# Queries loaded two chunks ahead and a group's first keys used last: an attention and expert kernel on one Trainium2 core

## The chip, the cores and the metric

The kernel runs on one core of one Trainium2 chip. The metric is device time in microseconds (us) of one launch. A core has a matrix engine (PE, with its weight loads shown apart as PEld), a vector engine (DVE), a scalar engine (ACT), a general engine (POOL) and SyncE (SP), which here issues nearly all DMA transfers. Each engine works through its own instructions in order.

## The reference, cut to what matters

The input `x` has 2048 tokens of 512 features. It is normalised (`xn`), and the output is `x + attention(xn) + experts(xn)`. Attention is the part that the change touches: 16 heads, each with two sets of queries and keys of depth 16 and one set of values of depth 32, a causal mask, two softmaxes.

```python
q = (query @ Wq).reshape(bsz, tgt_len, 2 * H, D)      # k likewise, then rotary on both
v = (query @ Wv).reshape(bsz, tgt_len, H, 2, D)
...
def causal_attn_pair(q, k, v1, v2, mask, scale):
    s = jnp.einsum('bthd,bshd->bhts', q, k) * scale
    s = jnp.where(mask, s, NEG)
    a = jax.nn.softmax(s, axis=-1)
    o1 = jnp.einsum('bhts,bshd->bthd', a, v1)
    o2 = jnp.einsum('bhts,bshd->bthd', a, v2)
    return jnp.concatenate([o1, o2], axis=-1)
...
attn = irfft((rfft(attn1) - lambda_full * rfft(attn2)) * filt)   # along the tokens
attn = attn * rsqrt(mean(attn * attn) + EPS) * rms_weight * (1.0 - LAMBDA_INIT)
return attn @ Wout
```

The expert part is a gated two-layer network: every token goes through a shared expert and through the two of eight routed experts that its gate chooses.

## The kernel before

Three stages follow each other. The opening normalises, projects to queries, keys and values, turns queries and keys by the rotary angles, routes the tokens, and writes queries and keys to two arrays in device memory, `parts[0]` and `parts[1]`. `middle` computes all of attention and nearly all of the expert work. `ending` does the filter along the tokens, the normalisation, the last projection and the sum.

**Groups, chunks, units.** `middle` works on two heads at a time, a group `g`, of which there are 8. A group has four chunks of 512 queries, taken from the last to the first: `qc` = 3, 2, 1, 0 (list `turns`, line 989). Because of the mask, chunk `qc` needs only the keys 0 to 512(qc + 1). Keys are kept in four column blocks `c` of 512 keys, each with a tile per head. A block holds four key tiles of 128, numbered `kb`, so `kb // 4` is the block. A unit is one head against one `kb`: two matmuls (line 831) into PSUM, then an exponential on ACT (line 844). `units` (lines 805 to 818) gives the order inside a chunk: first `LEAD[qc]` whole key tiles (0, 0, 2, 6 for the four chunks) and the first tile of the diagonal, then the rest of the diagonal, whose masking POOL does (line 853), then the whole tiles that are left. A chunk `qc` = 3 has 29 units, the others 21, 13 and 5, and 68 make a group.

**The order of the work.** All engines run in the order in which the program is written (`manual_schedule`). The loop at line 1038 takes four units at a time. `burst` issues the score matmuls of two of them; the product with the values (line 875), the sums of the last chunk (line 901), and one or more steps of expert work (`work`, line 1026, from the generator `experts`, line 626) follow, in the same instruction stream of PE. Expert weights are fetched by SP (line 151) as soon as the matmuls that used a buffer are issued.

**Loads of queries and keys.** `load_queries` (line 739) issues 8 transfers of 64 KB into two tiles, one per head; a tag has two buffers. `load_keys` (line 728) issues 4 transfers of 128 KB, two per head; each writes the same 32 source rows twice, through a source with a leading dimension of 2. Block 0 has four buffers, two groups' worth; blocks 1, 2 and 3 have two. Before the loop (lines 997 to 1000) SP gets all four blocks of group 0 and the queries of its first chunk. After that, at the start of every chunk, `burst` (lines 1008 to 1014) has SP load the next chunk's queries, and then one block of the next group's keys, `(qc + 1) % 4`: block 0 in chunk 3, block 3 in chunk 2, block 2 in chunk 1 and block 1 in chunk 0. SP takes these in turn with everything else in its stream, and it waits where a buffer is still being read. Eight completion semaphores serve SP's transfers in rotation, so that a transfer also waits for the one issued eight before it.

Of the kernel before, what the change touches and what calls it, by code (L numbers as in the profile page):

```python
# [9 lines left out]
F32R = mybir.dt.float32r  # L10
# [9 lines left out]
P = 128  # L20
# [5 lines left out]
QC = 512  # L26
NQC = T // QC
TQ = QC // P
NH = 16
NG = NH // 2  # L30
# [4 lines left out]
LEAD = (0, 0, 2, 6)  # L35
# [35 lines left out]
def block_kernel(  # L71
# [220 lines left out]
    with ExitStack() as pools:  # L292
        def pool(name, bufs, **kw):
            return pools.enter_context(tc.tile_pool(name=name, bufs=bufs, **kw))
# [219 lines left out]
        qp, ep = pool("qk", 2), pool("early", 2)  # L514
# [78 lines left out]
    def middle(general):  # L593


        with ExitStack() as pools:
# [8 lines left out]
            def pool(name, bufs, **kw):  # L605
                return pools.enter_context(tc.tile_pool(name=name, bufs=bufs, **kw))

            kp, qp, pp = pool("k", 2), pool("q", 2), pool("prob", 6 if general else 8)
# [118 lines left out]

            def load_keys(g, c):
                for h in (2 * g, 2 * g + 1):
                    k = kp.tile([P, QC], F32R, tag=f"k{c}", name="kS", bufs=4 if c == 0 else 2)  # L730
                    for s in range(2):
                        src = parts[1][2 * h + s, :, :, c * QC : (c + 1) * QC].rearrange("a d t -> (a d) t")
                        nc.sync.dma_start(
                            k[64 * s : 64 * s + 64, :].bitcast(F32),
                            src.unsqueeze(0).to_broadcast([2, 2 * D, QC]),
                        )
                    keys[h, c] = k

            def load_queries(g, qc):
                for h in (2 * g, 2 * g + 1):  # L740
                    q = qp.tile([P, QC], F32R, tag=f"q{h % 2}", name="qS")
                    for s in range(2):
                        for rep in range(2):
                            r = 64 * s + 32 * rep
                            nc.sync.dma_start(
                                q[r : r + 32, :].bitcast(F32),
                                parts[0][2 * h + s, rep : rep + 2, :, qc * QC : (qc + 1) * QC].rearrange("a d t -> (a d) t"),
                            )
                    queries[h, qc] = q
# [48 lines left out]
            class Chunk:  # L798
# [6 lines left out]
                def units(self):  # L805


                    d = self.qc * TQ
                    for kb in [*range(LEAD[self.qc]), d]:
                        for h in range(2):  # L810
                            yield [(h, kb, 0, 0, QC)]
                    for h in range(2):
                        yield [(h, d + 1, P, 0, 3 * P), (h, d + 3, 3 * P, 3 * P, P)]
                    last = [(h, d + 2, 2 * P, 2 * P * h, 2 * P) for h in range(2)]
                    yield from ([part] for part in last) if general else [last]
                    for kb in range(LEAD[self.qc], d):
                        for h in range(2):
                            yield [(h, kb, 0, 0, QC)]

# [44 lines left out]
                def values(self, kb):  # L864

                    if self.done == 0:
                        self.o = vps.tile([P, QC], F32, tag="o", name="ps_o")
                    self.done += 1
                    first, self.ended = self.done == 1, self.done == (self.qc + 1) * TQ
                    for h in range(2):  # L870
                        v0 = 64 * self.g + 32 * h
                        pt, off = self.probs[h, kb]
                        for s in range(2):
                            r = 64 * h + 32 * s
                            nc.tensor.matmul(  # L875
                                self.o[r : r + 32, off:], vd[:, kb, v0 : v0 + 32], pt[:, s, :],
                                start=first, stop=self.ended, skip_group_check=True,
                            )
                    if self.ended:
                        self.o_sb = ap.tile([P, QC], F32, tag="o_sb", name="o_sb")  # L880
                        nc.scalar.copy(self.o_sb, self.o)
# [107 lines left out]
            turns = [(g, qc) for g in range(NG) for qc in reversed(range(NQC))]  # L989
            stream = []  # L990
            for n, turn in enumerate(turns):
                chunk = Chunk(*turn)
# [3 lines left out]
            ex = experts()  # L996
            for c in range(NQC):
                load_keys(0, c)
                if c == 0:
                    load_queries(0, NQC - 1)  # L1000
            worked, begun, summed, held = 0.0, -1, 0, []
            todo, closing, closed, shared, ready, folding = [], [], [], [], [], None

            def burst(units):
                nonlocal begun
                found = []
                for n, chunk, unit in units:
                    if n > begun:
                        begun = n
                        if n + 1 < len(turns):  # L1010
                            load_queries(*turns[n + 1])

                        if chunk.g + 1 < NG:
                            load_keys(chunk.g + 1, (chunk.qc + 1) % NQC)
                    found += chunk.scores(unit)
                return found

# [20 lines left out]
            for i in range(0, len(stream), 4):  # L1038
                units = stream[i : i + 4]
                found = burst(units[:2])  # L1040
                n, ended = values()
                for c in closing:
                    c.sums()
                    summed += 1
                if n < 2 and not closing:

                    work()
                found += burst(units[2:])
                while todo:
                    ended += values()[1]  # L1050
# [20 lines left out]
                if any(masked(*u[1:]) for u in units) or not shared:  # L1071
                    steps = 0
                elif any(masked(*u[1:]) for u in stream[i + 4 : i + 8]):
                    steps = 1 if ready or units[0][1].g == NG - 1 else 0
                else:
                    steps = 2
# [269 lines left out]
    with tc.If(nc.values_load(more[0:1, 0:1], min_val=0, max_val=1) > 0):  # L1346

        with tc.tile_pool(name="before_more", bufs=1) as gap, tc.tile_pool(name="more", bufs=2) as mp, tc.tile_pool(
            name="more_ps", bufs=3, space=PSUM
# [24 lines left out]
    with tc.If(flag > 0) as cmp:  # L1374
        middle(False)
        ending()
    with cmp.Else():
        middle(True)
        ending()
# [103 lines left out]
```

## Time and profile before

| What | Value |
|---|---|
| median of 3 runs | 1334.18 us (1333.29 to 1334.27) |
| the profiled execution's own time | 1336.14 us |
| its span | 1334.3 us |
| PE busy | 1305.5 us, 98% of the span |
| DVE busy | 1007.7 us, 76% |
| ACT busy | 690.5 us, 52% |
| POOL busy | 620.3 us, 46% |
| key loads `kS<-parts_k` | 128 transfers of 128 KB |
| query loads `qS<-parts_q` | 256 transfers of 64 KB |
| expert weights `w<-in_wex_dram` | 132 transfers of 704 or 768 KB |

Times in the profile are counted from the start of the span. `middle`'s first score matmul stands at 254.0 us and its last at 1199.7 us. A busy PE in this profile means that an instruction is in it; a wait of PE for a semaphore is idle time, and the profile says which engine or transfer ended it. The trace also holds, for each transfer, when SP issued it and when its last part landed. "PEclk" is the clock that PE was granted, as a share of full speed.

### The profile page before, as it was taken

Reading aid. Unit: us, or ns where it says so; the run is one execution under the profiler, and the core shown is the slowest. Engines: PE = TensorE matmul, PEld = TensorE weight load, DVE = VectorE, ACT = ScalarE, POOL = GpSimd, SP = SyncE. Lnnn points to the kernel's source line nnn. Section 1 sums busy time; section 2 is a strip of 40 time slices with the busy share of each in tenths; the row PEclk is TensorE's granted clock in tenths of the full one; section 3 lists DMA queues with packets and bytes.
Section 4 is the critical chain, followed back from the end, with each engine's and each line's share of the span. In section 5 each row is a group of like instructions: output and inputs, shape, how many; then the busy total and the mean of one; then the engine's idle time right before and its main releaser. Section 6 shows DMA issues by size and latency. Waiting matters only on the chain.

```text
span 1334.3 us, 20914 instructions
## 1 busy us (share of the span) xinstructions
PE 1305.5 (98%) x7554; PEld 598.5 (45%) x7554; DVE 1007.7 (76%) x1316; ACT 690.5 (52%) x848; POOL 620.3 (46%) x639
## 2 busy tenths in 40 slices
PE   7999999999999999999999999999999999999998
PEld 3444444434343444444445444444544443445544
DVE  7049883277777868778987988888798869876784
ACT  2311110265666566666666666666666657662231
POOL 0002331012131233215985976894598666741774
PEclk9999999999999999999999999999999999999999
DMA  9405773201210023235566666566666667878998
GB/s 371 184 16 163 201 205 102 89 16 32 66 63 22 29 78 93 77 111 160 169 186 202 183 196 188 149 215 191 170 199 189 191 186 271 314 266 304 190 222 188
DMA packets 82058, 215.07 MB, mean 161 GB/s; under 512 B 12964, under 2 KB 13416, under 8 KB 81688
## 3 DMA queue, kind: packets, MB, share of 16 engines
q1 hardware_dynamic: 69224, 186.47, 43.9%
q0 software_dynamic: 11056, 22.78, 8.7%
q10 hardware_dynamic: 1664, 4.38, 1.0%
q8 instruction: 63, 1.03, 0.4%
q14 instruction: 51, 0.42, 0.1%
HBM read 170.48 MB, written 43.10 MB: 160 GB/s over the span
## 4 chain that ended last, share of the span: by engine, by line
PE 64%; POOL 8%; DMA 5%; issue 2%; DVE 2%; ACT 0%; SPq 0%; POOLq 0%; DVEq 0%; ACTq 0%
PE ps_o L875 17%; PE ps_s L831 12%; PE wh L244 8%; PE xy L214 6%; PE xh L181 5%; PE xg L181 5%; PE wy L283 4%; POOL res L1138 3%; DMA res<-ysh 2%; PE ps_sum L901 2%; DMA w<-in_wex_dram 1%; PE ps_x L167 1%; POOL pt L853 1%; DVE sum L892 1%; PE ps_ot L913 1%
## 5 line engine op out<-in xcount | busy, mean ns | idle before, releaser
L892 DVE TENSOR_TENSOR sum<-sum,pt 128x1024 f32<-128x1024 f32 (+2 forms) x576 | 628.7, 1140 | 30.4 <-POOL pt L853 13.6
L844 ACT ACTIVATE pt<-ps_s 128x1024 f32<-128x1024 f32 x544 | 527.3, 1022 | 182.5 <-PE ps_s L831 127.3
L853 POOL TENSOR_SCALAR_AFFINE_SELECT pt<-pt 128x256 f32<-128x256 f32 (+1 forms) x224 | 164.4, 756 | 368.4 <-ACT pt L844 342.9
L875 PE MATMUL ps_o<-pt,vd 128*32 128x512 f32 (+3 forms) x2560 | 267.7, 534 | 1.9 <-POOL pt L853 1.9
L831 PE MATMUL ps_s<-qS,kS 64*128 64x512 f32 (+3 forms) x1280 | 204.5, 407 | 1.6 <-DVEq L1346 1.2
L831 PEld LDWEIGHTS ps_s<-qS,kS 64*128 64x128 f32 x1280 | 97.5, 185 | 177.3 <-issue 96.7
L244 PE MATMUL wh<-xnT,w 128*128 128x512 f32 (+1 forms) x352 | 150.4, 574 | 0.0
L875 PEld LDWEIGHTS ps_o<-pt,vd 128*32 128x32 f32 x2560 | 67.2, 109 | 123.3 <-issue 105.9
L495 POOL DMA_INDIRECT who<-pairs,slot x32 | 33.8, 1055 | 171.3 <-DVE pairs L492 104.3
L542 PE MATMUL ps_x<-xnT,wqk_sb 128*128 128x512 f32 x256 | 110.5, 593 | 0.0
L244 PEld LDWEIGHTS wh<-xnT,w 128*128 128x128 f32 x352 | 64.1, 190 | 72.6 <-issue 56.5
L214 PE MATMUL xy<-w,uT 128*128 128x512 f32 (+3 forms) x240 | 94.6, 599 | 1.2 <-DVE rcp L916 1.2
L181 PE MATMUL xh<-w,xT 128*128 128x352 f32 (+1 forms) x320 | 90.4, 477 | 4.0 <-DMA w<-in_wex_dram 3.2
L181 PE MATMUL xg<-w,xT 128*128 128x352 f32 (+1 forms) x320 | 88.6, 468 | 0.0
L930 POOL TENSOR_TENSOR vd<-o_n 128x128 f32<-128x128 f32 x60 | 58.1, 986 | 53.8 <-DVE o_n L921 53.7
L542 PEld LDWEIGHTS ps_x<-xnT,wqk_sb 128*128 128x128 f32 x256 | 48.4, 190 | 60.6 <-issue 60.6
L283 PE MATMUL wy<-w,ws 128*128 128x512 f32 x160 | 74.8, 603 | 0.0
L559 ACT CAST hi<-turned 128x1024 fp32r<-128x1024 f32 x16 | 16.7, 1045 | 93.9 <-DVE turned L557 59.3
L1138 POOL DMA_INDIRECT res<-ys,slot x32 | 53.3, 1667 | 23.7 <-DMA res<-ysh 11.7
L181 PEld LDWEIGHTS xh<-w,xT 128*128 128x128 f32 (+1 forms) x320 | 48.3, 178 | 31.0 <-issue 9.3
L181 PEld LDWEIGHTS xg<-w,xT 128*128 128x128 f32 (+1 forms) x320 | 46.6, 174 | 34.4 <-issue 14.8
L377 PE MATMUL ps_tv<-wv_sb,xnT 128*128 128x512 f32 x128 | 59.8, 620 | 0.7 <-ACT xnT L374 0.7
(252 smaller groups left out, 1368.4 us busy)
## 6 DMA issues: line engine op xcount, KB each, us to landing
w<-in_wex_dram SPq DMA_DIRECT2D x88, 704.0 KB
w<-in_wex_dram SPq DMA_DIRECT2D x44, 768.0 KB
kS<-parts_k SPq DMA_DIRECT2D x128, 128.0 KB
qS<-parts_q SPq DMA_DIRECT2D x256, 64.0 KB
ys<-y_sb SPq DMA_DIRECT2D x34, 256.0 KB
parts_q<-hi SPq DMA_DIRECT2D x32, 256.0 KB
parts_k<-hi SPq DMA_DIRECT2D x16, 256.0 KB
parts_k<-turned SPq DMA_DIRECT2D x16, 256.0 KB
```

The costliest lines, as they stand in the source:

```text
L181: nc.tensor.matmul(dst[r, :], xT[:, c, r], w[:, c * FI : (c + 1) * FI], start=(c == 0), stop=(c == NE - 1), skip_group_check=True,)
L214: nc.tensor.matmul(y[r, :], uT[:m, ic, r], w[:m, ic * E : (ic + 1) * E], start=(ic == 0), stop=(ic == NF - 1), skip_group_check=True,)
L244: nc.tensor.matmul(dst, w_sb[o // WUP][o % WUP // WONE][:, o % WONE : o % WONE + P], x[:, c, :], start=(c == 0), stop=(c == NE - 1),)
L283: nc.tensor.matmul(y, us[i][:, t * P : (t + 1) * P], w_sb[i // NF][2][:, i % NF * E : (i % NF + 1) * E], start=(i == 0), stop=(i == SCH - 1),)
L377: nc.tensor.matmul(pv, xnT[:, c, t * P : (t + 1) * P], wv_sb[:, c, :], start=(c == 0), stop=(c == NE - 1))
L542: nc.tensor.matmul(ps[:, i, :], wqk_sb[st, qk][:, i, c, :], xnT[:, c, cols], start=(c == 0), stop=(c == NE - 1),)
L831: nc.tensor.matmul(to, k, queries[2 * g + h, qc][r, off : off + w], start=True, stop=not general)
L844: nc.scalar.activation(pt[:, :, used], ps[:, :, used], AF.Exp, scale=SCALE)
L853: nc.gpsimd.affine_select(out=part, in_=part, pattern=[[0, part.shape[1]], [1, P]], compare_op=ALU.is_ge, fill=0.0, base=0, channel_multip ...
L875: nc.tensor.matmul(self.o[r : r + 32, off:], vd[:, kb, v0 : v0 + 32], pt[:, s, :], start=first, stop=self.ended, skip_group_check=True,)
L892: nc.vector.tensor_add(to, to, pt)
L1138: nc.gpsimd.indirect_dma_start(out=came[k], out_offset=None, in_=ys, in_offset=bass.IndirectOffsetOnAxis(ap=slot[:, step - 2, order[k] : o ...
```

## The change

Queries: three buffers per tag instead of two, and at the start of chunk `n` SP loads the queries of chunk `n + 2` instead of `n + 1`. The queries of the second chunk are loaded ahead of the loop, after key block 1.

Keys: block 0 has two buffers like the others. In a chunk `qc` = 3 the whole key tiles are taken in the order 4 to 11, then 0 to 3, so that block 0 is the last that the chunk uses, from its 22nd unit on. Block 0 of a group is loaded at the start of that group's own chunk 3 (for group 0 ahead of the loop, as before) and no longer at the start of chunk 3 of the group before. The other blocks are loaded where they were. The number of buffers for keys and queries together stays at 14.

```diff
             def load_keys(g, c):
                 for h in (2 * g, 2 * g + 1):
-                    k = kp.tile([P, QC], F32R, tag=f"k{c}", name="kS", bufs=4 if c == 0 else 2)
+                    k = kp.tile([P, QC], F32R, tag=f"k{c}", name="kS")
...
             def load_queries(g, qc):
                 for h in (2 * g, 2 * g + 1):
-                    q = qp.tile([P, QC], F32R, tag=f"q{h % 2}", name="qS")
+                    q = qp.tile([P, QC], F32R, tag=f"q{h % 2}", name="qS", bufs=3)
...
                     d = self.qc * TQ
-                    for kb in [*range(LEAD[self.qc]), d]:
+
+                    kbs = [*range(TQ, d), *range(TQ)] if self.qc == NQC - 1 else [*range(d)]
+                    for kb in [*kbs[: LEAD[self.qc]], d]:
                         for h in range(2):
                             yield [(h, kb, 0, 0, QC)]
...
-                    for kb in range(LEAD[self.qc], d):
+                    for kb in kbs[LEAD[self.qc] :]:
                         for h in range(2):
                             yield [(h, kb, 0, 0, QC)]
...
             for c in range(NQC):
                 load_keys(0, c)
-                if c == 0:
-                    load_queries(0, NQC - 1)
+                if c < 2:
+                    load_queries(0, NQC - 1 - c)
...
                         begun = n
-                        if n + 1 < len(turns):
-                            load_queries(*turns[n + 1])
-
-                        if chunk.g + 1 < NG:
-                            load_keys(chunk.g + 1, (chunk.qc + 1) % NQC)
+                        if n + 2 < len(turns):
+                            load_queries(*turns[n + 2])
+
+                        c = (chunk.qc + 1) % NQC
+                        g = chunk.g + (c > 0)
+                        if 0 < g < NG:
+                            load_keys(g, c)
                     found += chunk.scores(unit)
```

## The prediction

> **What bounds the kernel now.** I read the page's busy times first, then the stage between 254 and 1205 us, then PE's waits in it.
>
> ```profile
> PE 1305.5 (98%) x7554; PEld 598.5 (45%) x7554; DVE 1007.7 (76%) x1316; ACT 690.5 (52%) x848; POOL 620.3 (46%) x639
> ```
>
> ```profile
> 254.00:1205.00 951.00, 943.57 (x6428) 425.50 (x6432) 771.95 (x898) 614.91 (x733) 513.66 (x543) 1.00 0.48 150
> ```
>
> In the second fence the first number after the window is its length, the next PE's busy time: 7.4 us of 951 idle. PE sets the time of this stage, and each us that it comes to wait is a us of the kernel. The waits of PE in that window are few:
>
> ```profile
> PE xh L181 <- DMA w<-in_wex_dram: 3.2, 2, 2.1
> PE ps_o L875 <- POOL pt L853: 1.9, 3, 1.4
> PE ps_s L831 <- DVEq L1346: 1.2, 1, 1.2
> PE xy L214 <- DVE rcp L916: 1.2, 1, 1.2
> ```
>
> No row says that PE waited for queries (qS) or keys (kS). So the change has no wait to remove there; the question is whether it makes one. For this I read SP's order of transfers around a group's end, here group 3's chunk 0 and group 4's chunk 3, and where PE starts on the latter:
>
> ```profile
> 713.25 8.74 SPq L745 DMA_DIRECT2D qS<-parts_q  x8
> 722.04 2.20 SPq L733 DMA_DIRECT2D kS<-parts_k  x4
> ```
>
> ```profile
> 724.91 0.73 PE L831 MATMUL ps_s<-qS,kS 64*128 64x512 f32 x4
> ```
>
> The columns are start, length, engine and line. The four kS transfers of 722 us are block 1 of group 4, issued at the start of the short chunk 0 (5 units), because chunk 1 was the last to read the old block 1. Group 4's first scores come 2.9 us later. Today they read block 0, loaded a hundred us before.
>
> **What the Trainium skill says.** "DMA: Bandwidth & Descriptors", section "Why a DMA increments its semaphore by 16 and not by 1": a transfer uses as many of the 16 DMA engines as divide its slowest dimension on both sides, up to 16. A key load's source has a leading dimension of 2, hence two engines. The trace agrees. While SP's queue held keys alone, from about 228 us, the rate stayed near 50 GB/s, in slices of 0.65 us (the peaks are stores that POOL issued):
>
> ```profile
> GB/s 44 47 22 91 32 50 50 47 47 50 50 50 50 50 54 50 41 28 25 47 54 340 114 50 50 54 47 50 173 284 50 76 57 44 50 50 211 246 50 50
> ```
>
> 128 KB at 50 GB/s is 2.6 us, and the landing records of that load stand 2.6 us apart (232.2, 234.8, 237.4 us). Four take some 10.5 us, however free the other engines are. The same page, "Queues, rings and completion order", has each DMA engine take its queue's work in order, so a block of keys also holds up the first two engines for every transfer behind it. "TensorE: Matmul & The Clock Gate", "Part 1: The HAM clock gate", says that an idle window of about 3.4 us halves PE's clock and a busy one restores it. The trace has one case, at the only wait of PE for weights:
>
> ```profile
> 1092.50:1096.50 4.00, 1.03 (x5) 0.19 (x3) 3.86 (x6) 1.05 (x2) 2.57 (x2) 0.92 0.50 129
> 1096.50:1102.50 6.00, 5.81 (x18) 2.20 (x18) 0.67 (x3) 0.53 (x2) 3.65 (x4) 0.50 0.52 154
> ```
>
> The third number from the right is the granted clock: after 3.15 us of idleness, 6 us at 0.50, that is 3 us lost on top.
>
> **The change part by part, against the profiled 1336.14 us (span 1334.3; 0.15% above the median of 1334.18).**
>
> *Queries two chunks ahead.* From the trace's landing records the tightest queries before are those of each group's chunk 3, ready for the first head 2.1 to 8.7 us ahead of use. They were never late, so nothing is gained: 0. SP's stream keeps 8 query transfers at each chunk start, with other contents, waiting for the same matmuls: the buffer they take was that of the chunk just finished, as now. Only the last load (8 transfers at 1170.6 us) moves away and 8 come in ahead of the loop. There block 1 keeps its place (landed 240.7, used from 254.0); blocks 2 and 3 slip by about 1.5 us of query data (8 x 0.19 us, the spacing of query landings), from 252.4 and 264.5 us, against a use at 269.6 and 276.4. Hidden by 10 us or more; without that cover, at most the 1.5 us.
>
> *Block 0 in two buffers, loaded in its own chunk 3.* This adds a wait of SP on the matmuls of the chunk 0 just ended, but the queries in front of it wait for the same ones. Behind it stand a result store and the down weights (w2), as before: every chunk 3 but the last had four kS there already. Its use comes at the 22nd unit. Laid over the trace, block 0 would land 2.9 us (group 4) to 19.6 us (group 1) before that, more after any delay of PE: 0. In group 7 the load is new in its place. Behind it a w2 transfer, which landed at 1106.2 us for a use at 1111.6, comes some 10.5 us later, at about 1117. By itself that would cost 5 us. The delay below moves the use to about 1121, so I put 0.
>
> *Block 1 first.* This is the step that counts. With order 4 to 11, then 0 to 3, the first two units of chunk 3 read block 1, one head each. Block 1 is still loaded at the start of chunk 0, behind 8 query transfers. It used to be needed from the 9th unit on (key tile 4), with 2.8 to 11.6 us to spare for the second head. Now it is needed by the 1st and 2nd. PE executes in order, so the values product, the sums and the expert work behind those two units wait as well. The stall is the landing of the second head's keys less the start of the second unit, both from the trace:
>
> group 1: 381.0 - 375.8 = 5.2; group 2: 503.6 - 497.3 = 6.3; group 3: 616.3 - 608.6 = 7.7; group 4: 738.0 - 725.2 = 12.8; group 5: 854.4 - 841.3 = 13.1; group 6: 975.7 - 963.0 = 12.7; group 7: 1092.3 - 1079.6 = 12.7. Sum 70.5 us. With 0.1 us each from landing to matmul (1094.71 to 1094.84 at the weights' wait), 71 us. Group 0 has its block early. The later groups stall longer because expert weights are on the queue.
>
> *The clock.* Seven stalls of over 5 us. The one case cost 3 us; by the page a release takes one to two windows of 3.4 us at half clock, so 1.7 to 3.4 us each. I take 2.6: 18 us.
>
> *What comes back.* The weights' wait at 1092.8 to 1096.7 falls into group 7's stall: 3.15 + 3 = 6 us. The short waits inside chunks 3 (ACT xT 0.7 at 614, DVE rcp 1.2 at 847, POOL pt 1.9) go, as those engines catch up: 3.5 us. Late next is PE itself again.
>
> *Sum.* 71 + 18 - 6 - 3.5 = 79.5, on the profiled time 1416, on the median 1334.2 + 79.5 = 1414 us. Instruction counts on all engines are unchanged.
>
> **Rivals.**
> (a) *Shorter stalls.* In the later groups the second head's keys needed 8 us for two transfers (729.9 to 738.0), not 5.2, as weights that SP issued behind them were moving too. Where PE's stall holds those weights back, about 3 us less in each of four groups, and the clock at its low end (-6): 1414 - 12 - 6 = 1396. For it: weights are issued when PE has read the old ones. Against: most were issued before the stall begins (726.3 us for 724.9, freed by matmuls at 722.5).
> (b) *Longer ones.* Clock at its high end (+6), no recovery of short waits (+4), w2 late in group 7 (+5): 1429.
> (c) *Faster.* If block 1 landed before the chunk, only the relief would be left: block 0 no longer queued ahead of other groups' needs, and the wait of 6 us for weights at 1094 gone. 1334.2 - 6 = 1328. It decides if the four kS of block 1 take less than the 2.7 to 8 us between their issue and the first scores; 128 KB would have to land in under 0.7 us in the later groups, where the trace shows 2.6. Or the compiled program would have to move the load; its SP order in the changed program still has it behind the queries at the start of chunk 0, and its first score matmuls of a group still wait for it.
> (d) *No difference.* Slower and faster parts would have to cancel, or the order in the chunk would have to be other than the diff says. Nothing in the instruction order supports it.
>
> **How the numbers follow.** Main case with (a) and (b) as its ends: 0.94. (c) 0.03, (d) 0.03. A measurement of this kernel tells about 0.2% (2.7 us) from no change. Faster 0.03, same 0.03, slower 0.94. The range, 1395 to 1431, is (a) to (b) and a little beyond; what it leaves out is (c), (d) and a misjudged stall.
>
> **What would show it.** In the profile after: PE ps_s waiting for kS, seven times, some 70 us in sum, 5 to 13 us each, right at the start of chunks 3 of groups 1 to 7 and none in group 0; a granted clock of 0.5 for some us after each; no wait of xh for weights near group 7; PE's busy time up by the clock's share, other engines' busy times unchanged. I am wrong if PE doesn't wait there, if the keys are issued earlier than the queries of chunk 0, or if kS transfers take far less than 2.6 us.

## The result and the profile after

| | before | changed |
|---|---|---|
| median | 1333.74 us (4 runs) | 1416.89 us (1415.65 to 1420.32, 4 runs) |
| ratio to before | | 1.0628, 95% interval 1.0608 to 1.0647 |
| span of the profiled execution | 1334.3 us | 1418.6 us |

The change makes the kernel 83 us slower. One run of the kernel before (1866.59 us, granted clock 0.66) and one of the kernel with the keys ahead of the queries (1650.37 us, 0.75) were in a slower state and are left out below. First the busy times of the changed kernel's page, and the row of the granted clock in 40 equal slices of the span:

```profile
PE 1330.0 (94%) x7554; PEld 606.0 (43%) x7554; DVE 1008.5 (71%) x1316; ACT 690.9 (49%) x848; POOL 630.8 (44%) x639
...
PEclk9999999999999999989997999799989989999999
```

The instruction counts are those of before. PE's busy time grew by 24.5 us though it does the same work, and the clock row has dips at near regular distances. DVE and ACT are unchanged. The stage that held 7.4 us of idle PE time now has 66. In this row the window is followed by its length, the busy times of PE, PEld, DVE, ACT and POOL, the granted clock, the DMA engines' busy share and GB/s, and the idle time is the length less PE's busy time:

```profile
254.00:1288.00 1034.00, 968.22 (x6425) 432.79 (x6428) 773.04 (x898) 615.28 (x733) 520.25 (x542) 0.96 0.45 137
```

The waits of PE between 370 and 1170 us (columns: total us, times, longest) say for what:

```profile
PE ps_s L833 <- DMA kS<-parts_k: 52.9, 21, 5.0
PE ps_s L833 <- issue: 9.0, 3, 4.1
PE ps_o L877 <- POOL pt L855: 1.8, 2, 1.6
PE xh L181 <- ACT xT L169: 0.7, 1, 0.7
```

Line 833 is the score matmul (831 before). It waits for keys, which it did nowhere before, for 61.9 us: the three waits of the second row stand between waits of the first at the same places. The wait of xh for weights is gone (xh and xg are an expert's two input products, xy its output product). One group's start, on PE, shows how a wait goes. This is group 4, whose block 1 SP issued at 747.2 us, behind the queries:

```profile
738.70 8.42 SPq L745 DMA_DIRECT2D qS<-parts_q  x8
747.16 2.38 SPq L733 DMA_DIRECT2D kS<-parts_k  x4
```

```profile
751.99 0.47 PE L833 MATMUL ps_s<-qS,kS 64*128 64x512 f32 x1 [1.56 <-DMA kS<-parts_k]
754.52 0.79 PE L833 MATMUL ps_s<-qS,kS 64*128 64x512 f32 x1 [2.06 <-DMA kS<-parts_k]
758.94 0.76 PE L833 MATMUL ps_s<-qS,kS 64*128 64x512 f32 x1 [3.63 <-DMA kS<-parts_k]
763.66 0.76 PE L833 MATMUL ps_s<-qS,kS 64*128 64x512 f32 x1 [3.96 <-DMA kS<-parts_k]
764.35 4.49 PE L877 MATMUL ps_o<-pt,vd 128*32 128x512 f32 x32
```

The first two units of the chunk are four matmuls, and each waits for the next of the four key transfers. PE gets on at 764.35 us. The 32 instructions of the values product behind took 2.36 us at this place before (from 725.58 us) and take 4.49 here. The reason is the clock, the third number from the right in these windows of the same execution:

```profile
757.00:764.40 7.40, 1.50 (x6) 0.62 (x10) 0.00 (x0) 0.00 (x0) 0.00 (x0) 0.50 0.71 176
764.40:770.00 5.60, 5.60 (x61) 2.81 (x64) 0.00 (x0) 1.61 (x2) 0.00 (x0) 0.50 0.27 79
770.00:776.00 6.00, 6.00 (x49) 3.04 (x45) 4.21 (x7) 3.68 (x5) 2.95 (x4) 1.00 0.34 63
```

For 5.6 us after the stall PE works all the time at half clock, then at full.

### The profile page after: what moved, and what is told of

It reads as the page before. It is cut to its first block, busy times and chain, and to the rows that moved or that the text cites. A ratio compares the mean times of both kernels' runs of the same rounds, so it can differ in the third digit from the quotient of the medians.

```text
span 1418.6 us, 20879 instructions
## 1 busy us (share of the span) xinstructions
PE 1330.0 (94%) x7554; PEld 606.0 (43%) x7554; DVE 1008.5 (71%) x1316; ACT 690.9 (49%) x848; POOL 630.8 (44%) x639
## 4 chain that ended last, share of the span: by engine, by line
PE 57%; DMA 13%; POOL 9%; issue 2%; SPq 1%; DVE 0%; ACT 0%; POOLq 0%; ACTq 0%; DVEq 0%
PE ps_o L877 16%; PE ps_s L833 11%; PE wh L244 7%; DMA kS<-parts_k 7%; PE xy L214 5%; PE xg L181 4%; PE xh L181 4%; PE wy L283 4%; DMA w<-in_wex_dram 3%; POOL res L1142 3%; PE ps_sum L903 2%; DMA res<-ysh 1%; POOL pt L855 1%; PE ps_ot L915 1%; PE ps_x L167 1%
## 5 line engine op out<-in xcount | busy, mean ns | idle before, releaser
L877 PE MATMUL ps_o<-pt,vd 128*32 128x512 f32 (+3 forms) x2560 | 281.4, 558 | 2.7 <-POOL pt L855 2.6
L833 PE MATMUL ps_s<-qS,kS 64*128 64x512 f32 (+3 forms) x1280 | 217.5, 411 | 63.5 <-DMA kS<-parts_k 52.9
L833 PEld LDWEIGHTS ps_s<-qS,kS 64*128 64x128 f32 x1280 | 101.9, 186 | 247.2 <-issue 142.0
L877 PEld LDWEIGHTS ps_o<-pt,vd 128*32 128x32 f32 x2560 | 70.1, 113 | 133.5 <-issue 115.7
L542 PE MATMUL ps_x<-xnT,wqk_sb 128*128 128x512 f32 x256 | 110.5, 593 | 0.0
L918 DVE RECIPROCAL rcp<-ps_st 128x16 f32<-128x16 f32 x32 | 8.3, 260 | 137.4 <-PE ps_st L916 137.4
L181 PE MATMUL xh<-w,xT 128*128 128x352 f32 (+1 forms) x320 | 86.8, 462 | 0.8 <-ACT xT L169 0.7
```

The lines of the kernel that those rows point to most:

```text
L181: nc.tensor.matmul(dst[r, :], xT[:, c, r], w[:, c * FI : (c + 1) * FI], start=(c == 0), stop=(c == NE - 1), skip_group_check=True,)
L542: nc.tensor.matmul(ps[:, i, :], wqk_sb[st, qk][:, i, c, :], xnT[:, c, cols], start=(c == 0), stop=(c == NE - 1),)
L833: nc.tensor.matmul(to, k, queries[2 * g + h, qc][r, off : off + w], start=True, stop=not general)
L877: nc.tensor.matmul(self.o[r : r + 32, off:], vd[:, kb, v0 : v0 + 32], pt[:, s, :], start=first, stop=self.ended, skip_group_check=True,)
```

## The experiments

The theory: block 1 became the first block that chunk 3 reads and lands too late, because it is issued late and moves on two DMA engines; each stall also costs some slow clock. The rivals: the query loads do it; the two-buffer block 0 does it; the growth of PE's busy time is something other than the clock. Ratios are to the kernel before as it ran beside each experiment (medians of 1334.4 to 1335.4 us).

**The keys' part alone.**

```diff
-                    q = qp.tile([P, QC], F32R, tag=f"q{h % 2}", name="qS", bufs=3)
+                    q = qp.tile([P, QC], F32R, tag=f"q{h % 2}", name="qS")
...
-                        if n + 2 < len(turns):
-                            load_queries(*turns[n + 2])
+                        if n + 1 < len(turns):
+                            load_queries(*turns[n + 1])
```

> The changed kernel with the queries put back (two buffers, loaded one chunk ahead); the keys' part of the change stays. Theory (block 1 is now the first block that a group's chunk 3 reads and lands 5 to 13 us too late): the stalls stay, 1417 us, within 4. Rival (the third query buffers and the longer reach of the query loads crowd SP's queue, so that keys and weights come late): the time falls back towards 1334, at least half of the 83 us goes.

Measured: 1417.08 us, ratio 1.0617 (1.0598 to 1.0636), PE busy 1329.5 us. That is the changed kernel's time within the noise: beside the keys' part, the queries' part costs nothing and brings nothing, and all of the loss comes from the keys' part.

**Block 2 first.**

```diff
-                    kbs = [*range(TQ, d), *range(TQ)] if self.qc == NQC - 1 else [*range(d)]
+                    kbs = [*range(2 * TQ, d), *range(TQ, 2 * TQ), *range(TQ)] if self.qc == NQC - 1 else [*range(d)]
```

> The changed kernel with one list reordered: chunk 3 takes key tiles 8 to 11, then 4 to 7, then 0 to 3, so that block 2 (loaded two chunks earlier) is read first and block 1 from the 9th unit on, as before the change. Loads, buffers and SP's order are those of the changed kernel. Theory: no wait of PE for keys is left, the clock stays at full, 1334 us (1328 to 1340). Rival (the two-buffer block 0 or the query loads cost the time): stays above 1375.

Measured: 1346.49 us, ratio 1.0093 (1.0075 to 1.0111). The reordered list takes away 70 of the 83 us, so the order in the chunk is the cause of these, and neither block 0's buffers nor the queries are. The expectation missed by 6 us at its upper end. PE's waits in this kernel, in the middle stage:

```profile
PE xy L214 <- DMA w<-in_wex_dram: 7.5, 1, 7.5
PE xh L181 <- DMA w<-in_wex_dram: 3.5, 2, 2.9
PE ps_o L877 <- POOL pt L855: 1.9, 3, 1.4
```

No keys, but a new wait of xy for down weights, 7.5 us long. It stands in group 7's chunk 3, where SP has this order (same kernel):

```profile
1082.53 17.81 SPq L745 DMA_DIRECT2D qS<-parts_q  x8
1100.38 2.19 SPq L733 DMA_DIRECT2D kS<-parts_k  x4
1102.68 1.98 SPq L226 DMA_DIRECT2D ys<-y_sb  x1
1104.91 4.54 SPq L151 DMA_DIRECT2D w<-in_wex_dram  x5
```

The kS there are block 0 of group 7, new in this place. By the landing records the last of them came at 1117.3 us and the first of the weights behind at 1119.4, 14.5 us after its issue; before, the weights at this place needed 4.8 us. PE started on them at 1119.48, and its clock stayed at half until 1125.4, 6 us in which it did what full clock does in 3:

```profile
1119.50:1125.40 5.90, 5.90 (x16) 1.80 (x16) 0.00 (x0) 0.51 (x1) 0.00 (x0) 0.50 0.14 55
```

So the wait cost some 7.5 + 3 us of the 12; the rest isn't traced.

**Only that block cut up.** In the kernel with block 2 first, block 0 of group 7 is loaded in transfers of 32 rows, two for each of before.

```diff
+                        if (g, c) == (NG - 1, 0):
+                            for r in (64 * s, 64 * s + 32):
+                                nc.sync.dma_start(k[r : r + 32, :].bitcast(F32), src)
+                        else:
...
```

> The kernel with block 2 read first, with one block of keys alone, block 0 of group 7, cut into transfers of 32 rows. Theory (its four transfers hold two DMA engines in front of group 7's down weights, which cost that kernel 7.5 us of waiting and 5 us of slow clock): the wait of xy for weights goes, the wait of xh for weights at 1094 us stays; 1334 us (1331 to 1338). Rival (the down weights are late from the queries in front of them): 1344 or more.

Measured: 1338.02 us, ratio 1.0020 (1.0011 to 1.0028), just at the upper end of what was expected. The wait of xy is gone, and that of xh stays:

```profile
PE xh L181 <- DMA w<-in_wex_dram: 4.0, 2, 2.9
PE ps_o L881 <- POOL pt L859: 1.9, 3, 1.4
```

Eight of the 12 us went with four transfers' shape; the queries in front of the weights are as before, so the rival falls. It lies 3 us above the kernel before (1335.37 us beside it). The wait of xh is 0.8 us longer than there, and its trace has a period of 3.4 us at half clock at 255 us that the others lack; the rest stays open.

**Keys ahead of the queries.**

```diff
-                        if n + 2 < len(turns):
-                            load_queries(*turns[n + 2])
-
                         c = (chunk.qc + 1) % NQC
                         g = chunk.g + (c > 0)
                         if 0 < g < NG:
                             load_keys(g, c)
+                        if n + 2 < len(turns):
+                            load_queries(*turns[n + 2])
```

> The changed kernel with the two loads at a chunk's start exchanged: the keys are issued ahead of the 8 query transfers, so some 4 us earlier in groups 1 to 3 and some 8 us earlier in groups 4 to 7. Theory: the stalls fall from 63 us to about 23 (0, 1, 4, 5, 4, 4, 6 us), with perhaps half of the slow-clock time; 1364 us (1350 to 1380). Rival (the keys' own transfer time alone sets the landing, the queries ahead of them are cheap): 1405 or more.

Measured: 1362.92 us (median of three runs), ratio 1.0223 (1.0201 to 1.0245). The wait for keys, 61.9 us in the changed kernel, is

```profile
PE ps_s L833 <- DMA kS<-parts_k: 16.9, 9, 2.7
```

The place in SP's queue was worth 54 us. That the rest is the transfers' own time isn't shown by this run; the kernels with cut transfers below bear it out.

**Useless matmuls in the stall.**

```diff
+FILL = (0, 23, 29, 37, 54, 46, 51, 55)
...
+                    if qc == NQC - 1 and g > 0 and unit[0][:2] == (0, TQ):
+                        for i in range(FILL[g]):
+                            nc.tensor.matmul(ps[:, i % 2, :C_TRI], ident, cst, start=True, stop=True)
```

> The changed kernel with useless matmuls (identity by 224 constant columns, into PSUM that the scores then overwrite) ahead of the first unit of chunk 3 in groups 1 to 7: 23, 29, 37, 54, 46, 51 and 55 of them, some 0.19 us each, a little less than each stall. They add work to the outputs' computation that changes nothing in it. Theory (some 27 us of the loss is PE's halved clock after each stall): the stalls stay as filled time, the clock stays at full, 1390 us (1385 to 1400). Rival (the growth of PE's busy time has another cause, such as contention): 1417 or above.

Measured: 1440.13 us, ratio 1.0792 (1.0773 to 1.0811). By the time alone this is the rival's range, but the edit was mis-sized, so the time can't decide. In the groups of this kernel, with shapes kept apart,

```profile
L831 PE MATMUL ps_s<-cst 128*128 128x224 f32 x590 | 112.9, 353 | 0.0
```

295 calls became 590 instructions, so that a filling took 0.38 us and not 0.19, and the filling outlasted every stall. Even so its busy time answers the rival. No wait for keys was left, and the clock stayed at full through the middle stage:

```profile
254.00:1310.00 1056.00, 1052.10 (x7042) 535.48 (x7046) 774.02 (x899) 614.96 (x734) 520.28 (x542) 1.00 0.43 135
```

PE's busy time, 1413.1 us, is that of the kernel with cut transfers below (1302.6) plus 110.5. The filling accounts for that (112.9, in part at the same time as the matmuls beside it), so with the clock at full the growth is gone.

**Half the filling.** `FILL = (0, 11, 14, 18, 26, 23, 25, 27)`.

> As the run with useless matmuls, with 11, 14, 18, 26, 23, 25 and 27 of them: there each took 0.38 us and not 0.19 (two PE instructions each), so the filling was longer than the stalls and set the time itself. Theory (slow clock): the filling now fits in the stalls, the clock stays at full, and what is left of the loss is the stalls alone: 1334.7 + 62.7 (stalls of the changed kernel) - 6 (the weights' wait and its slow clock) = 1391 us (1386 to 1398). Rival (PE's busy time grows for another cause): 1415 or more.

Measured: 1409.06 us (1405.16 to 1410.05), ratio 1.0560 (1.0539 to 1.0581). Adding work made the kernel 8 us faster, as the clock theory has it, but by less than expected: it lies between the theory's range and the rival's. In the middle stage the time at half clock fell from 89 us to 14 us in the traces. The expectation had taken all of PE's growth in busy time as lost time. Part of it lies inside the stalls, where matmuls run slow between two waits and cost nothing. Take the stretch from the start of the last matmul ahead of a group's first scores (the filling not counted) to the start of the first behind its first two units. Summed over groups 1 to 7, the trace has 83.1 us for the changed kernel, 78.9 here and 8.6 with cut transfers. So the stalls are 70 us at nearly full clock and 75 with the slow clock in them.

**Block 1 a group early.** The queries go back to two buffers; block 1 gets four.

```diff
-                    k = kp.tile([P, QC], F32R, tag=f"k{c}", name="kS")
+                    k = kp.tile([P, QC], F32R, tag=f"k{c}", name="kS", bufs=4 if c == 1 else 2)
...
-                        if 0 < g < NG:
+                        if 0 < g < NG and c != 1:
                             load_keys(g, c)
+                        if chunk.qc == 2 and chunk.g + 1 < NG:
+                            load_keys(chunk.g + 1, 1)
```

> The changed kernel with the queries put back (two buffers, one chunk ahead) and the four key tiles that this frees given to block 1, which is then loaded at the start of the chunk 2 of the group before. 14 tiles in all, as in both kernels; no keys are loaded in the short chunk 0. Theory: no wait for keys, the weights' wait of the last groups goes with the keys that stood in front of them in chunk 0 of group 6; 1328 us (1325 to 1333). Rival (block 0 of group 7 in front of the weights costs its 12 us here too): 1338 to 1346.

Measured: 1354.39 us, ratio 1.0142 (1.0120 to 1.0164). Both expectations missed. No wait for keys is left, but these came:

```profile
PE ps_s L833 <- DMA qS<-parts_q: 8.2, 6, 3.0
...
PE xh L181 <- DMA w<-in_wex_dram: 4.4, 1, 4.4
PE xy L214 <- DMA w<-in_wex_dram: 3.0, 1, 3.0
```

Eight key transfers in a row at the start of chunk 2 made all that followed late. In group 3, SP finished issuing the queries of chunk 0 at 702.3 us and block 2 began then:

```profile
691.76 10.54 SPq L745 DMA_DIRECT2D qS<-parts_q  x8
702.35 2.36 SPq L733 DMA_DIRECT2D kS<-parts_k  x4
```

In the kernel before, the same kS began at 696.3 us. The 6 us went on to the next queries, those of group 4's chunk 3, which landed at 729.7 us and not 723.6, and had only 1 to 2 us to spare there. Two chunks of lead, which this kernel doesn't have, might have covered that; no run tried it.

**Cut transfers in the changed kernel.**

```diff
-                        nc.sync.dma_start(
-                            k[64 * s : 64 * s + 64, :].bitcast(F32),
-                            src.unsqueeze(0).to_broadcast([2, 2 * D, QC]),
-                        )
+                        for r in (64 * s, 64 * s + 32):
+                            nc.sync.dma_start(k[r : r + 32, :].bitcast(F32), src)
```

> The changed kernel with each key transfer of 128 KB cut into two of 64 KB whose source has 32 rows (no leading dimension of 2), so that by the Trainium skill each uses 16 DMA engines; order and buffers unchanged. Theory (two engines make the keys late): a block lands some 6 us after its first issue and not 13 to 14, the stalls fall to 0 in groups 1 to 3 and to 2 or 3 us in groups 4 to 7; 1336 us (1328 to 1346). Rival (the place in SP's queue is the cause, and more transfers make it worse): 1390 or more.

Measured: 1329.99 us (1329.27 to 1331.52, 8 runs), ratio 0.9965 (0.9953 to 0.9977). All 87 us go with the shape of the key transfers, and the kernel is a little faster than before as well. The completion records show the difference in engines: of the changed kernel's 128 key transfers 122 have three increments of their semaphore, one 0.4 us after the issue and two as the data lands; of the 256 cut ones 254 have sixteen. The same place as above, group 4's block 1:

```profile
712.98 4.77 SPq L743 DMA_DIRECT2D qS<-parts_q  x8
717.80 3.68 SPq L734 DMA_DIRECT2D kS<-parts_k  x8
```

The eight land between 719.8 and 722.9 us, some 0.45 us apart, 1.9 us after the last issue; PE wants them at 724.65. The queries ahead of them are also through sooner (4.8 us against 8.4), as nothing in front of them stands on two engines. In the changed kernel it was 16 us from the first key issue to the last landing. PE's waits in the middle stage are back to small ones:

```profile
PE ps_o L875 <- POOL pt L853: 2.6, 4, 1.4
PE ps_s L831 <- DVEq L1348: 1.3, 1, 1.3
PE xy L214 <- DVE rcp L916: 0.9, 1, 0.9
PE xh L181 <- ACT xT L169: 0.7, 1, 0.7
PE ps_s L831 <- DMA kS<-parts_k: 0.3, 1, 0.3
```

**Cut transfers in the kernel before.** The same edit.

> The kernel before with the same cut of the key transfers, nothing else. Theory: its one wait of PE for weights (3 us and 3 us of slow clock) goes, as keys no longer hold up two of the engines: 1328 us (1326 to 1331). Rival (that wait comes from the volume of the weights): no change, 1334.

Measured: 1330.10 us, ratio 0.9964 (0.9951 to 0.9977). The wait for weights is gone here too, so it was the keys in front of them and not the weights' volume. The longest entry of PE's waits in the middle stage is now

```profile
PE ps_o L873 <- POOL pt L851: 2.7, 4, 1.4
```

With the cut, the order of before and the order of the change give the same time, with PE busy for 98% of either span.

**Cut transfers for block 1 alone,** in the changed kernel (`if c == 1` in the edit above).

> The changed kernel with block 1's loads alone cut into transfers of 32 rows. Theory: the 62 us of waits at the starts of chunk 3 go but for about 3 us in each of groups 4 to 7, where the queries in front are still held up by block 2's two-engine transfers; with the slow clock of those, and up to 12 us for group 7's weights behind block 0, 1350 us (1338 to 1362). Rival (all key transfers share in the loss, not block 1's landing): above 1375.

Measured: 1348.96 us, ratio 1.0087 (1.0064 to 1.0111). PE waits 5.4 us for keys in all, and 3.7 us for down weights:

```profile
PE ps_s L837 <- DMA kS<-parts_k: 5.4, 9, 1.4
PE xy L214 <- DMA w<-in_wex_dram: 3.7, 1, 3.7
```

68 us go with the shape of block 1's transfers alone. The other 19 of the 87 go with the other blocks' shape, as the kernel with all of them cut shows; the wait for down weights is one place where they cost, and the rest isn't split up.

**Block 1 a group early, with cut transfers.** Both edits together.

> The kernel that loads block 1 a group early, which waited for queries and weights instead, with all key transfers cut into 32 rows. Theory (8 key transfers at the start of a chunk 2 hold two DMA engines for 21 us and pass their delay down the queue to the queries of the next chunks, which had only 2 us to spare): no wait for queries or weights, 1330 us (1327 to 1334), the same as the other kernels with cut transfers. Rival (the place of the loads in SP's stream is the cause): 1345 or more.

Measured: 1330.48 us, ratio 0.9956 (0.9943 to 0.9970), no wait for queries or weights in the middle stage. The 24 us that the early loads cost go with the shape of the key transfers as well.

## Why the prediction was right

The mechanism came as predicted: the waits, their places, the half clock behind them, and none in group 0. The sum was 79.5 us; the medians differ by 83 and the spans of the profiled executions by 84.3. In the prediction's own terms the 84.3 are 74.5 for stalls, plus 15.4 for the clock, less 5.6 for what comes back. The stalls were put too low by 3.5, the clock too high by 2.6, and the relief too high by 3.9. That the total is off by 4.8 and not by 7.4 is luck.

*The stalls.* Predicted 71 us. Measured as the stretches above, changed kernel less cut transfers: 5.6, 6.6, 8.4, 13.3, 14.1, 13.3, 13.2, together 74.5 us, of which 61.9 are idle and the rest matmuls between the waits. Each is 0.3 to 1.0 us longer than predicted. The lateness of a moved use could be read off a trace in which nothing waited. Rival (a), shorter stalls because weights are held back, didn't come.

*The clock.* Predicted 18 us for seven stalls. Between the spans of the changed kernel and of that with cut transfers (1418.6 and 1328.7) lie 89.9 us, 15.4 more than the stretches. The trace says the same another way. Behind the ends of the seven stalls the clock stayed at half for 3.4, 3.2, 4.9, 5.6, 5.6, 5.4 and 2.8 us, together 30.9, and half of that is lost: 15.5 us, or 2.2 per stall and not 2.6. The filling gained 8 us in the median and 15 between the two profiled executions; the one is the fastest of its four runs and the other the slowest.

The Trainium skill, "TensorE: Matmul & The Clock Gate", section "Part 1: The HAM clock gate", has windows of about 3.4 us by which the clock is set, and the trace's periods of half clock agree (6.8, 6.8, 10.2, 17.1, 17.1, 17.1 and 13.7 us). The prediction's "one to two windows" is an estimate from that page. On one point the measurement goes further than the page's "idle window": in the 3.4 us ahead of the seven drops of the clock PE was busy for 1.2, 0.7, 0.7, 1.4, 0.0, 1.3 and 0.5 us. So a stall that is broken up by single matmuls halved the clock too, and in group 1 no gap was longer than 2.2 us. The clock came back only after 3.4 us in which PE never idled.

*What comes back.* Predicted 6 + 3.5 us (its three short waits add up to 3.8). The weights' wait and its slow clock went. The short waits mostly didn't: in the middle stage POOL's rose from 1.9 to 2.6 and xT's stayed at 0.7; only rcp's 1.2 is gone. The step that failed is that other engines' catching up would clear them. The kernel with cut transfers, which has no stalls, is 5.6 us shorter than the one before (1328.7 and 1334.3).

*Block 0.* Put at 0 because the delay moves the use: right, the changed kernel has no wait of xy for weights. But "By itself that would cost 5 us" was too low. With the stalls gone it cost 7.5 us and 3 us of slow clock, as the weights came 13 us later than before, not 10.5. With a harmless order the change would still lose 12 us, as the kernel with block 2 first does.

*Queries.* Put at 0, and shown by the keys' part alone and by the two kernels with cut transfers, one with the longer lead and one without (1329.99 and 1330.10 us). But "never late" held by 1 to 2 us only, as the early block 1 showed.

*The DMA engines.* The Trainium skill, "DMA: Bandwidth & Descriptors", section "Rules for kernel authors", says that a broadcast of c copies as the leading dimension keeps a transfer on at most c engines. The trace agrees, with the two increments per key transfer as the data lands against sixteen for a cut one, and the cut made the difference of 87 us in the changed kernel. Rival (c) named the point from which it decides, under 0.7 us for 128 KB; with cut transfers it is 0.9 us for two of 64 KB and the queries ahead are faster by 4 us, and the kernel does become faster than before, at 1330 us against the 1328 worked out.

## What to carry to other kernels

When a consumer's order changes, list for each block its first use beside its landing: the block that is now first may be the one that is loaded last. Here, where PE had been busy for 98% of the span, each us of such lateness counted whole, and some 2 us of slow clock per stall came on top. Before lead or buffers are added, see how many DMA engines the transfer uses; here a broadcast as the leading dimension made a small load hold up what was queued behind it.

## What was unexpected

How much transfers suffer from those in front: down weights took 14.5 us from issue to landing behind four key transfers and 4.8 us at the same place without them. One matmul call with an identity in f32 became two PE instructions of 0.19 us spacing (224 columns). And some 55 us of useless matmuls (288 instructions) made a kernel faster.
